# Layer 2 of a two-layer network: the loads of B and C become steps of the written plan, and one pair of states changes engine

## The chip, the core and the metric

The kernel runs on one core of one Trainium2 chip. The core has five engines that work side by side, each through its own queue of instructions in order: PE (TensorE, matrix products and transposes), DVE (VectorE), ACT (ScalarE), POOL (GpSimd) and SP (SyncE, which here only issues DMAs). The metric is the device time of one execution in microseconds (us); less is better.

## The reference

The input is an image batch of 4 x 192 x 128 x 128. Two layers follow one another, each with a residual sum over a group norm. Layer 1 is a convolution block in a fractional Fourier domain. It takes the first 1400 us or so, and the change doesn't touch it. Layer 2 is a selective state space model over the 16384 pixels of each image, with 384 channels and 16 states per channel:

```
xz = einsum(seq, in_proj_w);  xs, z = split(xz)
u = silu(causal_conv(xs, 4 taps))
dt, Bm, Cm = split(einsum(u, x_proj_w));  dt = softplus(dt_proj(dt))
for every token t:
    h = h * exp(dt_t * A) + (dt_t * u_t) * B_t        # 384 x 16 numbers
    y_t = sum over the 16 states of h * C_t
out = out_proj((y + u * Dp) * silu(z))
```

## The kernel before

Layer 2 cuts each image into 32 chunks of T = 512 tokens, 128 chunks in all. The 384 channels are three tiles of 128 partitions (j = 0, 1, 2), and the 16 states are eight pairs (sg = 0 to 7). One *group* is one j and one pair: 24 groups per chunk, k = 8 j + sg. The main loop runs over all groups of all chunks in order, `order` in the code, at position `pos`.

For one group the work is:

- the *decay* exp(dt A), one ACT activation per state (`decay`, L906)
- the *product* dt u B, made in one of three ways that the table `KINDS` names, a letter for each j and sg. V: DVE multiplies a copy of dt u in PSUM by B (`product`, L927). O: POOL multiplies both states at once (`inputs`, L938). P: dt u is transposed on PE (`turned`, L947), ACT scales the transposed blocks by B, which is a value per partition there (`scale`, L955, four activations per state), and PE transposes them back (`turned_back`, L970, four transposes per state)
- the *scan*, h = h x decay + product along the tokens, one DVE instruction per state (L984)
- the multiplication by C of both states at once on POOL (L997, hc)
- the sum over states on PE, by transposes that accumulate in PSUM (`sums`, L1010), three groups later (`LAG`)

After each group's scans SP issues a 1 KB DMA that keeps the last column of h for the next chunk (`carry`, L995).

The buffers matter. h has three (a scan of group k + 3 needs the buffer of group k: its hc and its carry DMA must be done). The PSUM ring `op` has three: each state uses one slot, for a V product, a turned-back P product, or the decay of an O state (`decay_there`, issued three states ahead). Decays of V and P states go to a ring of seven in SBUF (`early`). The scaled tiles dbT have four buffers, db two. For B and C there is one buffer per pair and kind, b0 to b6 and c0 to c7. Each holds two rows of 512 tokens spread to 128 partitions, 512 KB to move. B is not loaded for pairs that are P for all three j (sg 3 and 7).

All other work of a chunk, from the loads of x to the output projection, is written out by hand in `PLAN` (L560): a step is (position, phase, name, arguments). Positions count groups from the chunk's first scan. So the steps of the next chunk at -24 to -1 fall beside the scans of this one, at position + 24, and those from 24 on fall beside the scans of the next. The phases of one position are S, A, M, L: S first, then a turned-back product and the sums; A; then POOL's db product of two groups later; then the first scan, the next products, M, the second scan, and L. Within one engine the order of issue is the order of execution.

Steps named below: `evacuate` copies the sum of one j to SBUF (ACT), `turn` transposes it (PE), `gate` multiplies by silu(z) (DVE, L1042), `project_out` (PE) and `add_x` (DVE, L1056) finish the chunk. `to_tokens`, `moments`, `normed`, `to_channels`, `channels`, `conv`, `proj_z`, `silu_u`, `silu_z` and `proj_x` prepare a later one; `xd_out` and `dbc_out` store B and C to DRAM; `proj_dt`, `softplus` and `dt_u` (POOL, L853) make dt and dt u; `turn_b` and `b_out` make the transposed B.

The loads of B and C are the exception: they aren't in the plan. `load_bc` is called at the end of fixed positions, for pairs 0 to 4 in the last five groups of the chunk before and for pairs 5 to 7 in the first three groups:

```
if k >= NGR - BCL and n + 1 < total:
    load_bc(n + 1, k - (NGR - BCL))
if k < NG - BCL and n:
    load_bc(n, k + BCL)
```

Of the kernel before, what the change touches and what calls it, by code (L numbers as in the profile page):

```python
# [10 lines left out]
F32 = mybir.dt.float32  # L11
# [3 lines left out]
ALU = mybir.AluOpType  # L15
# [3 lines left out]
S = 128  # L19
# [4 lines left out]
L = S // 2 + 1  # L24
# [6 lines left out]
T = 512  # L31
# [90 lines left out]
def layer0(tc, x, xmid, st2, w):  # L122
# [432 lines left out]

BUFS = 7, 3

KINDS = ("VOPPVVOP", "VOVPVVPP", "VOVPVPOP")

PLAN = (  # L560
    (-35, "M", "load_x"), (-34, "L", "to_tokens", 0), (-33, "S", "to_tokens", 1),
    (-32, "S", "moments", 0), (-32, "L", "moments", 1), (-32, "L", "rstd"), (-30, "A", "shift"),
    (-30, "A", "normed", 0), (-30, "A", "normed", 1), (-30, "M", "to_channels", 1),
    (-28, "S", "to_channels", 0), (-28, "S", "channels", 0), (-27, "M", "conv", 0, 0),
    (-27, "L", "channels", 1), (-26, "A", "conv", 1, 0), (-25, "S", "conv", 1, 1),
    (-25, "A", "conv", 1, 2), (-21, "S", "conv", 0, 1), (-21, "L", "conv", 0, 2),
    (-20, "S", "silu_u", 0), (-20, "A", "silu_u", 1), (-19, "L", "conv", 2, 0),
    (-18, "S", "conv", 2, 1), (-18, "L", "conv", 2, 2), (-16, "L", "silu_u", 2),
    (-15, "A", "proj_z", 0), (-15, "M", "silu_z", 0), (-13, "M", "proj_x"), (-12, "S", "xd_out"),
    (-11, "M", "proj_dt"), (-10, "S", "dbc_out"), (-10, "A", "softplus", 0),  # L570
    (-10, "M", "softplus", 1), (-10, "M", "softplus", 2), (-10, "L", "turn_b"),
    (-10, "L", "b_out"), (-9, "L", "dt_u", 1), (-8, "L", "dt_u", 0), (-3, "L", "turned", 0),
    (-2, "M", "dtu_copy", 0), (-2, "L", "scale", 0, 6), (-1, "S", "scale", 0, 4),
    (0, "L", "scale", 0, 5), (1, "M", "scale", 0, 14), (2, "A", "scale", 0, 7),
    (3, "A", "scale", 0, 15), (4, "L", "turned", 1), (5, "M", "scale", 1, 6),
    (6, "S", "dtu_copy", 1), (7, "S", "scale", 1, 7), (7, "L", "dt_u", 2),
    (9, "M", "scale", 1, 14), (10, "M", "scale", 1, 13), (10, "L", "scale", 1, 15),
    (10, "L", "evacuate", 0), (10, "L", "proj_z", 1), (11, "M", "proj_z", 2),
    (11, "M", "silu_z", 1), (11, "M", "silu_z", 2), (11, "L", "scale", 1, 12),
    (11, "L", "turn", 0), (12, "L", "gate", 0), (13, "M", "dtu_copy", 2), (16, "M", "turned", 2),  # L580
    (17, "A", "scale", 2, 6), (17, "L", "scale", 2, 10), (18, "S", "scale", 2, 7),
    (18, "A", "evacuate", 1), (19, "S", "scale", 2, 14), (19, "A", "scale", 2, 11),
    (19, "L", "scale", 2, 15), (21, "A", "turn", 1), (21, "M", "gate", 1),
    (26, "M", "evacuate", 2), (28, "M", "load_xr"), (28, "L", "turn", 2), (30, "L", "gate", 2),
    (31, "S", "project_out", 0), (32, "L", "add_x", 0), (34, "S", "project_out", 1),
    (34, "L", "add_x", 1),
)


def layer1(tc, xmid, out, st2, w, n_tok=S * S):  # L590

    nc = tc.nc
    B = len(xmid)
    NCHUNK = n_tok // T
    G = 2
    LAG, BCL = 3, 5
    AHEAD, H = BUFS
    NBLK = T // 128

    with ExitStack() as ctx:  # L600
# [8 lines left out]
        bcp = pool("l1b", 1)  # L609
# [50 lines left out]
        for half in range(2):  # L660
            nc.sync.dma_start(
                out=wc[64 * half : 64 * (half + 1)], in_=w["taps"][half].partition_broadcast(64)
            )
        for part in range(2):
# [7 lines left out]
        xpT, dtT, dtb, cb, dp, woT, A = (  # L672
            const(k) for k in ("xpT", "dtT", "dtb", "cb", "dp", "woT", "A_log")
        )
# [8 lines left out]
        total = B * NCHUNK  # L683
        NG = NS // G
        NGR = NJ * NG
        got = [{} for _ in range(total)]
# [180 lines left out]
            )  # L867
            done(g, "bt")

        def load_bc(i, sg):  # L870

            g = got[i]
            if any(kinds[sg] != "P" for kinds in KINDS):
                t = g["b", sg] = bcp.tile([128, G, T], F32, name=f"b{sg}")
                nc.sync.dma_start(
                    out=t, in_=g["dbc"][0, sg * G : (sg + 1) * G, :].partition_broadcast(128)
                )
            t = g["c", "b", sg] = bcp.tile([128, G, T], F32, name=f"c{sg}")
            nc.sync.dma_start(
                out=t, in_=g["dbc"][1, sg * G : (sg + 1) * G, :].partition_broadcast(128)  # L880
            )

        def dtu_copy(n, j):

# [9 lines left out]
        def kind(k):  # L894
            return KINDS[k // NG][k % NG]

# [75 lines left out]
        def scans(pos, n, k, between):  # L972
            g = got[n]
            j, sg = divmod(k, NG)
            ch = n % NCHUNK
            if k == 0:
                g["carry"] = tp.tile([128, NJ, NS], F32, name="carry")
                g["before"], last["carry"] = last.get("carry"), g["carry"]
            db = g.pop(("db", k), None)
            h = scp.tile([128, G, T], F32, name="h", bufs=H)  # L980
            for q in range(G):
                st = sg * G + q
                s = G * pos + q
                nc.vector.tensor_tensor_scan(  # L984
                    h[:, q, :], das.pop(s), dbs.pop(s) if db is None else db[:, q, :],
                    0.0 if ch == 0 else g["before"][:, j, st : st + 1], ALU.mult, ALU.add,
                )
                product(s + 2)
                decay_there(s + 3)
                if q == 0:  # L990
                    turned_back(s + 3)
                    between()
                if s in turns:
                    early(turns[s] + AHEAD)
            nc.sync.dma_start(out=g["carry"][:, j, sg * G : (sg + 1) * G], in_=h[:, :, T - 1])  # L995
            hc = scp.tile([128, G, T], F32, name="hc", bufs=5)
            nc.gpsimd.tensor_tensor(hc, h, g["c", "b", sg], ALU.mult)  # L997
            g["hc", k] = hc

        def sums(n, k):  # L1000
# [53 lines left out]
        def add_x(n, t):  # L1054
# [6 lines left out]

        order = [(n, k) for n in range(total) for k in range(NGR)]
        does = dict(
            load_x=load_x, load_xr=load_xr, to_tokens=to_tokens, moments=moments, rstd=rstd, shift=shift,
            normed=normed, to_channels=to_channels, channels=channels, conv=conv, proj_z=proj_z,
            silu_u=silu_u, silu_z=silu_z, proj_x=proj_x, xd_out=xd_out, dbc_out=dbc_out, proj_dt=proj_dt, softplus=softplus, dt_u=dt_u,
            turn_b=turn_b, b_out=b_out, dtu_copy=dtu_copy, turned=turned, scale=scale,
            evacuate=evacuate, turn=turn, gate=gate, project_out=project_out, add_x=add_x,
# [14 lines left out]
        with tc.manual_schedule():  # L1083
            log_exp()
            for pos in range(first, 0):
                for phase in "SAML":
                    act(pos, phase)
                if pos == -8:
                    for sg in range(NG):
                        load_bc(0, sg)  # L1090
                if pos <= LAST:
                    yield pos == LAST
                if pos == LAST:
                    scp = pool("l1s", 4)
                    op = pool("l1o", 1)
                    ps2 = pool("l1q", 1, space=PSUM)
                    psa = pool("l1a", 3, space=PSUM)
                    banks.append(4)
                    group_norm(B - 1)
            inputs(*order[1])  # L1100
            for at in range(AHEAD):
                early(at)
            for s in range(2):
                product(s)
            decay_there(2)


            for pos, (n, k) in enumerate(order):
                j, sg = divmod(k, NG)
                act(pos, "S")  # L1110
                turned_back(G * (pos + 1))
                if pos >= LAG and sg != LAG:
                    sums(*order[pos - LAG])
                act(pos, "A")
                if pos + 2 < len(order):
                    inputs(*order[pos + 2])
                scans(pos, n, k, lambda: act(pos, "M"))
                act(pos, "L")
                if pos >= LAG and sg == LAG:
                    sums(*order[pos - LAG])  # L1120
                    add_skip(n, j)
                if k >= NGR - BCL and n + 1 < total:
                    load_bc(n + 1, k - (NGR - BCL))
                if k < NG - BCL and n:
                    load_bc(n, k + BCL)
            for pos in range(len(order), len(order) + end - NGR + 1):
                act(pos, "S")
                if pos < len(order) + LAG:
                    sums(*order[pos - LAG])
                for phase in "AML":  # L1130
                    act(pos, phase)
# [150 lines left out]
```

## Time and profile before

| | us |
|---|---|
| median of three runs | 11220.84 (11219.14 to 11226.6) |
| the profiled execution, its own time | 11219.08 |
| its span, first to last instruction | 11217.3 |
| granted TensorE clock, mean | 0.944 |
| hc on POOL (L997), one instruction | 2.367, 3072 times |
| scan on DVE (L984), one instruction | 1.267, 6144 times in four forms |
| V product on DVE (L927) | 0.675, 2560 times |
| carry DMA, issue to landing, median | 1.9 |
| loads of c and b, issue to landing, median | 6.0 and 5.0 |

In the rows of the profile, "L984 DVE" is the line of the code and the engine; the shapes are output <- input; "x" is a count; after the bar come the busy time in us and the mean length of one in ns; then the engine's idle time just before these instructions and what ended it. A wait list has one row for each engine, tile and releaser: the total in us, the number of times, and the longest. A timeline row begins with the start and the length in us, and ends in square brackets with the idle time ahead of it. A table of stretches has the stretch, its length, the busy time and the count of each engine, the granted clock, the mean busy share of the 16 DMA engines and the GB/s.

### The profile page before, as it was taken

The page shows a single profiled execution, that of the slowest core. Times are in us where ns is not written, and L with a number is a line of the kernel's source. Part 1 is how long each engine was busy: PE and PEld are TensorE (multiplying, and loading weights), DVE is VectorE, ACT ScalarE, POOL GpSimd, SP SyncE. Part 2 cuts the span into 40 slices and gives each one's busy share as a digit, 9 for nine tenths or more (in the row PEclk, how much of TensorE's full clock was granted, in tenths as well). Part 3 has the DMA queues.
Part 4 walks back from the last instruction along what each step waited for, and adds up shares of the span by engine and source line. Part 5 has one row for each costly group of instructions (what it writes and reads, how often), then busy time and mean ns, then how long its engine had stood idle before and what let it go on. Part 6 is the DMA issues. An engine that isn't in the chain of part 4 may idle for free. (4 is left out here: it accounts for less than half of the span.)

```text
span 11217.3 us, 171938 instructions
## 1 busy us (share of the span) xinstructions
PE 10022.3 (89%) x56050; PEld 7046.3 (63%) x56050; DVE 10265.6 (92%) x11587; ACT 9573.1 (85%) x20327; POOL 9223.7 (82%) x4214
## 2 busy tenths in 40 slices
PE   4777799999999999999999999999999999999998
PEld 2444366666666666666666666666666666666666
DVE  5667599999999999999999999999999999999999
ACT  2333299999999999999999999999999999999998
POOL 0000199999999999999999999999999999999998
PEclk8888799999999999999999999999999999999999
DMA  8886734334334334334344334344344344344343
GB/s 233 191 226 180 225 96 123 112 111 123 113 110 123 109 114 123 107 117 123 105 119 123 105 118 123 102 121 123 100 121 124 99 123 123 99 124 121 101 123 96
DMA packets 1357326, 1416.85 MB, mean 126 GB/s; under 512 B 920729, under 2 KB 972174, under 8 KB 1355790
## 3 DMA queue, kind: packets, MB, share of 16 engines
q1 hardware_dynamic: 1335950, 1342.94, 41.5%
q0 software_dynamic: 13312, 50.34, 1.4%
q10 hardware_dynamic: 7168, 12.59, 0.3%
q8 instruction: 446, 7.31, 0.3%
q14 instruction: 450, 3.69, 0.1%
HBM read 1230.12 MB, written 155.33 MB: 124 GB/s over the span
## 5 line engine op out<-in xcount | busy, mean ns | idle before, releaser
L997 POOL TENSOR_TENSOR hc<-h,c 128x1024 f32<-128x1024 f32 x3072 | 7218.1, 2367 | 691.6 <-DVE h L984 572.5
L984 DVE TENSOR_TENSOR_SCAN h<-da,carry,op 128x512 f32<-128x512 f32 x4712 | 5846.4, 1267 | 157.3 <-PE op L970 78.9
L906 ACT ACTIVATE da<-dt,c_A_log 128x512 f32<-128x512 f32 x4864 | 3394.9, 737 | 75.4 <-DVE h L984 68.0
L1010 PE MATMUL ps<-ident,hc 128*128 128x128 f32 x24576 | 3270.7, 281 | 5.7 <-POOL hc L997 4.8
L1010 PEld LDWEIGHTS ps<-ident,hc 128*128 128x128 f32 x24576 | 2919.1, 146 | 279.4 <-issue 257.4
L955 ACT ACTIVATE dbT<-ps,bT 128x128 f32<-128x128 f32 x9216 | 2547.7, 389 | 2.7 <-PE ps L947 2.7
L795 PE MATMUL ps<-s,wc 128*128 128x512 f32 x4608 | 2141.1, 596 | 57.1 <-ACT s L780 57.1
L970 PE MATMUL op<-ident,dbT 128*128 128x128 f32 x9216 | 1500.7, 288 | 612.3 <-DVE h L984 588.2
L970 PEld LDWEIGHTS op<-ident,dbT 128*128 128x128 f32 x9216 | 1137.6, 148 | 1004.8 <-ACT dbT L955 556.0
L927 DVE TENSOR_TENSOR op<-ps,b 128x512 f32<-128x512 f32 x2560 | 1727.2, 675 | 6.4 <-ACT ps L887 1.0
L984 DVE TENSOR_TENSOR_SCAN h<-op,carry,db 128x512 f32<-128x512 f32 x1240 | 1542.3, 1269 | 109.1 <-DMA carry<-h 51.3
L938 POOL TENSOR_TENSOR db<-dtu,b 128x1024 f32<-128x1024 f32 x640 | 1515.0, 2367 | 6.1 <-DVE nmr L638 6.1
L795 PEld LDWEIGHTS ps<-s,wc 128*128 128x128 f32 x4608 | 806.6, 191 | 761.2 <-issue 684.8
L906 ACT ACTIVATE op<-dt,c_A_log 128x512 f32<-128x512 f32 x1280 | 906.7, 708 | 219.8 <-DVE h L984 219.3
L1049 PE MATMUL ps<-yg,c_woT 128*96 128x512 f32 x1536 | 710.8, 599 | 2.1 <-ACT u L807 0.9
L692 ACT ACT_TABLE_LOAD x511 | 655.6, 1283 | 10.0 <-PEq L1272 0.7
L514 POOL DMA_DIRECT2D xmid<-xt x64 | 42.1, 658 | 585.6 <-DVE xt L510 557.1
L1049 PEld LDWEIGHTS ps<-yg,c_woT 128*96 128x96 f32 x1536 | 241.3, 163 | 429.7 <-issue 312.5
L853 POOL TENSOR_TENSOR dtu<-dt,u 128x512 f32<-128x512 f32 x384 | 489.9, 1276 | 0.0
L1019 ACT COPY yt<-ps 128x512 f32<-128x512 f32 x384 | 226.4, 590 | 283.0 <-PE ps L1010 282.2
L1025 PE MATMUL ps<-ddp,u 128*128 128x128 f32 x3072 | 446.1, 293 | 0.0
L205 DVE BATCH_NORM_STATS2 st<-xt 96x6 f32<-96x512 f32 x512 | 322.5, 677 | 104.5 <-DMA xt<-in_x 103.4
(173 smaller groups left out, 9609.5 us busy)
## 6 DMA issues: line engine op xcount, KB each, us to landing
c<-dbc SPq DMA_DIRECT2D x1024, 512.0 KB, 6.0
b<-dbc SPq DMA_DIRECT2D x768, 512.0 KB, 5.0
xt<-in_x SPq DMA_DIRECT2D x176, 768.0 KB, 8.4
xmid<-xt POOLq DMA_DIRECT2D x64, 768.0 KB, 6.1
xm<-xmid SPq DMA_DIRECT2D x128, 384.0 KB, 3.7
carry<-h SPq DMA_DIRECT2D x3072, 1.0 KB, 1.9
xr<-xmid SPq DMA_DIRECT2D x128, 384.0 KB, 4.9
out<-xr SPq DMA_DIRECT2D x128, 384.0 KB, 3.3
```

The source lines that it names most:

```text
L692: nc.scalar.preload_act_table_set("natural_log_exp_and_others")
L795: nc.tensor.matmul(g["c", j][0], wc[:, j, k, :], rhs, start=k == 0, stop=k == 5)
L853: nc.gpsimd.tensor_tensor(g["dtu", j], g["dt", j], g["u", j], ALU.mult)
L906: nc.scalar.activation(da, got[n]["dt", j], AF.Exp, scale=A[:, j, st : st + 1])
L927: nc.vector.tensor_tensor(dbs[s], g["dp", j][0], g["b", k % NG][:, q, :], ALU.mult)
L938: nc.gpsimd.tensor_tensor(db, _bc(g["dtu", j], 1, G), g["b", sg], ALU.mult)
L955: nc.scalar.activation(t[:, blk, :], g["tu", j][0][:, at], AF.Identity, scale=g["bT"][:, blk, st : st + 1],)
L970: nc.tensor.transpose(db[:, blk * 128 : (blk + 1) * 128], t[:, blk, :], ident)
L984: nc.vector.tensor_tensor_scan(h[:, q, :], das.pop(s), dbs.pop(s) if db is None else db[:, q, :], 0.0 if ch == 0 else g["before"][:, j, st ...
L997: nc.gpsimd.tensor_tensor(hc, h, g["c", "b", sg], ALU.mult)
L1010: nc.tensor.matmul(py[:, blk, :], hc[:, q, blk * 128 : (blk + 1) * 128], ident, start=first, stop=sg == NG - 1 and q == G - 1 and blk == N ...
L1049: nc.tensor.matmul(g["po", t][0][0:CH], woT[:, j, t * CH : (t + 1) * CH], g["yg", j], start=j == 0, stop=j == NJ - 1,)
```

## The change

Three things are edited together. `load_bc` is split into `load_b` and `load_c`, and each call becomes a step of the plan. In the plan before the loads ran at groups 19 to 23 and 0 to 2 (end of the position). In the new one, in positions from the chunk's first scan: b0 at -7; b2, b1, c0 at -6; c1, b4, c2, c3 at -4; b5 at -1; c4, c6 at 0; b6 at 1; c5 at 2; c7 at 5 (steps for b3 and b7 load nothing). One letter of `KINDS` goes from P to O: j = 1, sg = 6. So a chunk has six O, ten V and eight P pairs instead of five, ten and nine. And the order of nearly all other steps in the plan is new.

```diff
-KINDS = ("VOPPVVOP", "VOVPVVPP", "VOVPVPOP")
+KINDS = ("VOPPVVOP", "VOVPVVOP", "VOVPVPOP")
```

```diff
 PLAN = (
...
-    (-30, "A", "normed", 0), (-30, "A", "normed", 1), (-30, "M", "to_channels", 1),
-    (-28, "S", "to_channels", 0), (-28, "S", "channels", 0), (-27, "M", "conv", 0, 0),
...
-    (-18, "S", "conv", 2, 1), (-18, "L", "conv", 2, 2), (-16, "L", "silu_u", 2),
...
-    (-11, "M", "proj_dt"), (-10, "S", "dbc_out"), (-10, "A", "softplus", 0),
-    (-10, "M", "softplus", 1), (-10, "M", "softplus", 2), (-10, "L", "turn_b"),
-    (-10, "L", "b_out"), (-9, "L", "dt_u", 1), (-8, "L", "dt_u", 0), (-3, "L", "turned", 0),
-    (-2, "M", "dtu_copy", 0), (-2, "L", "scale", 0, 6), (-1, "S", "scale", 0, 4),
-    (0, "L", "scale", 0, 5), (1, "M", "scale", 0, 14), (2, "A", "scale", 0, 7),
...
-    (18, "A", "evacuate", 1), (19, "S", "scale", 2, 14), (19, "A", "scale", 2, 11),
-    (19, "L", "scale", 2, 15), (21, "A", "turn", 1), (21, "M", "gate", 1),
...
-    (31, "S", "project_out", 0), (32, "L", "add_x", 0), (34, "S", "project_out", 1),
-    (34, "L", "add_x", 1),
+    (-30, "M", "normed", 0), (-29, "S", "normed", 1), (-29, "M", "to_channels", 0),
+    (-29, "M", "channels", 0), (-26, "S", "conv", 1, 0), (-26, "S", "to_channels", 1),
...
+    (-17, "L", "conv", 2, 1), (-15, "A", "conv", 2, 2), (-15, "L", "proj_z", 0),
+    (-15, "L", "silu_z", 0), (-14, "M", "silu_u", 2), (-13, "M", "proj_x"), (-11, "S", "xd_out"),
+    (-10, "A", "dbc_out"), (-10, "A", "proj_dt"), (-10, "A", "softplus", 0),
+    (-10, "L", "softplus", 1), (-9, "S", "softplus", 2), (-9, "S", "turn_b"), (-9, "M", "b_out"),
+    (-9, "L", "dt_u", 0), (-7, "A", "load_b", 0), (-7, "L", "dt_u", 1), (-6, "S", "load_b", 2),
+    (-6, "S", "load_b", 1), (-6, "A", "load_c", 0), (-5, "M", "turned", 0),
+    (-4, "S", "load_c", 1), (-4, "S", "load_b", 4), (-4, "L", "load_c", 2),
+    (-4, "L", "load_c", 3), (-3, "S", "load_b", 3), (-2, "A", "scale", 0, 7),
+    (-2, "M", "dtu_copy", 0), (-2, "M", "scale", 0, 15), (-1, "S", "load_b", 5),
+    (-1, "M", "scale", 0, 6), (-1, "M", "scale", 0, 4), (0, "M", "load_c", 4),
+    (0, "L", "load_c", 6), (1, "S", "scale", 0, 5), (1, "M", "load_b", 6), (2, "A", "load_b", 7),
+    (2, "L", "load_c", 5), (3, "S", "scale", 0, 14), (5, "A", "turned", 1), (5, "A", "load_c", 7),
...
+    (18, "S", "scale", 2, 10), (18, "S", "scale", 2, 6), (18, "L", "evacuate", 1),
...
+    (21, "M", "turn", 1), (21, "M", "gate", 1), (25, "S", "load_xr"), (27, "A", "evacuate", 2),
+    (28, "L", "turn", 2), (31, "A", "gate", 2), (32, "M", "project_out", 0),
+    (33, "A", "add_x", 0), (34, "S", "project_out", 1), (35, "S", "add_x", 1),
 )
```

```diff
-        def load_bc(i, sg):
-            g = got[i]
+        def rows_of(i, name, sg):
+            t = got[i][name, sg] = bcp.tile([128, G, T], F32, name=f"{name}{sg}")
+            a = "bc".index(name)
+            nc.sync.dma_start(
+                out=t, in_=got[i]["dbc"][a, sg * G : (sg + 1) * G, :].partition_broadcast(128)
+            )
+
+        def load_b(i, sg):
             if any(kinds[sg] != "P" for kinds in KINDS):
...
+                rows_of(i, "b", sg)
+
+        def load_c(i, sg):
+            rows_of(i, "c", sg)
...
-                if pos == -8:
-                    for sg in range(NG):
-                        load_bc(0, sg)
...
-                if k >= NGR - BCL and n + 1 < total:
-                    load_bc(n + 1, k - (NGR - BCL))
-                if k < NG - BCL and n:
-                    load_bc(n, k + BCL)
```

## The prediction

> **What bounds the kernel now.** I read the page first, for the busy shares and the costliest groups; then the busy time over a steady stretch of layer 2; then the DVE's waits in that stretch; then the POOL's timeline over part of one chunk, to see where it is free.
>
> ```profile
> PE 10022.3 (89%) x56050; PEld 7046.3 (63%) x56050; DVE 10265.6 (92%) x11587; ACT 9573.1 (85%) x20327; POOL 9223.7 (82%) x4214
> ...
> L955 ACT ACTIVATE dbT<-ps,bT 128x128 f32<-128x128 f32 x9216 | 2547.7, 389 | 2.7 <-PE ps L947 2.7
> ...
> L970 PE MATMUL op<-ident,dbT 128*128 128x128 f32 x9216 | 1500.7, 288 | 612.3 <-DVE h L984 588.2
> ...
> L938 POOL TENSOR_TENSOR db<-dtu,b 128x1024 f32<-128x1024 f32 x640 | 1515.0, 2367 | 6.1 <-DVE nmr L638 6.1
> ```
>
> Shares over the whole span mix the two layers; layer 2 starts near 1400 us. Its steady stretch (busy us and counts of PE, PEld, DVE, ACT, POOL, then clock, DMA share, GB/s) and three pieces of one chunk:
>
> ```profile
> 2000.00:11000.00 9000.00, 8339.51 (x48363) 6001.20 (x48362) 8629.94 (x9622) 8448.74 (x18194) 8369.99 (x3760) 0.96 0.39 115
> 5063.00:5089.00 26.00, 25.64 (x151) 19.28 (x150) 21.26 (x21) 22.77 (x58) 23.02 (x10) 0.95 0.82 269
> 5089.00:5124.00 35.00, 33.42 (x176) 21.36 (x174) 34.96 (x38) 33.10 (x62) 31.16 (x14) 1.00 0.22 50
> 5124.00:5142.00 18.00, 13.80 (x93) 12.08 (x91) 17.53 (x27) 16.63 (x38) 17.34 (x10) 0.78 0.06 4
> ```
>
> The store of dbc is issued once per chunk, first at 1339.2 and last at 11097.6 us: 9758.4 / 127 = 76.84 us per chunk, so 9000 us are 117.1 chunks. Per chunk DVE is busy 8629.94 / 117.1 = 73.7 us, ACT 72.1, POOL 71.5 and PE 71.2. DVE, with 3.16 us idle, is the bound, and everything else is within 4% of it: only DVE's idle time can be won. What its idle time waited for, 2000 to 11000 us:
>
> ```profile
> DVE yg L1042 <- PE ps L1035: 105.1, 116, 1.3
> DVE h L984 <- PE op L970: 75.7, 188, 0.5
> DVE h L984 <- DMA carry<-h: 68.0, 89, 2.4
> DVE h L984 <- issue: 45.7, 52, 1.5
> DVE h L984 <- ACT dbT L955: 31.4, 24, 1.7
> DVE h L984 <- ACT da L906: 14.0, 26, 0.9
> DVE h L984 <- POOL hc L997: 10.4, 11, 2.1
> ```
>
> Divided by 117.1: the gate for PE 0.90 us per chunk, scans for a turned-back P product 0.65, for a carry DMA (which holds one of three h buffers) 0.58, unnamed 0.39, scaled tiles 0.27, decays 0.12, POOL 0.09; together 3.0. So nine tenths are waits for PE, ACT and DMA, not for POOL. Where POOL is free, groups 10 to 15 of one chunk:
>
> ```profile
> 5031.90 2.37 POOL L997 TENSOR_TENSOR hc<-h,c 128x1024 f32<-128x1024 f32 x1 [0.54 <-DVE h L984]
> 5035.51 2.35 POOL L997 TENSOR_TENSOR hc<-h,c 128x1024 f32<-128x1024 f32 x1 [1.24 <-DVE h L984]
> 5039.07 2.37 POOL L997 TENSOR_TENSOR hc<-h,c 128x1024 f32<-128x1024 f32 x1 [1.21 <-DVE h L984]
> 5043.14 2.36 POOL L997 TENSOR_TENSOR hc<-h,c 128x1024 f32<-128x1024 f32 x1 [1.69 <-DVE h L984]
> 5045.80 2.37 POOL L997 TENSOR_TENSOR hc<-h,c 128x1024 f32<-128x1024 f32 x1 [0.30 <-DVE h L984]
> ```
>
> These gaps add up to 4.98 us (3.42 in the next chunk), waiting for scans.
>
> **What the Trainium skill says.** "DMA: Bandwidth & Descriptors", Queues, rings and completion order: SP owns one ring on each DMA engine, and an engine takes descriptors in ring order. So a 1 KB carry issued behind 512 KB loads starts after them; the trace agrees, carries land after 1.9 us in the median and 7.6 at most. "GPSIMD Engine Reference", 3.1 Elementwise: about 2.6 cycles per element for a two-input operation at 1.2 GHz, an estimate of 2.2 us for 1024 elements; the trace has 2.37. "ScalarE: Activation LUTs", What ACT_TABLE_LOAD costs: 1283 ns a load and another 1380 of draining. The trace has the 1283, but the activation after the load of 5013.02 starts at 5014.32, so no draining shows; 1.28 us is the price.
>
> **The pair that changes kind (j=1, sg=6, from P to O).** Removed per chunk: two scales of four activations, 8 x 2547.7/9216 = 2.2 us of ACT, and eight transposes, 8 x 1500.7/9216 = 1.3 us of PE. ACT falls to 69.9 us, PE to 69.9. Added: one db product. Back to back they start 2.33 us apart in the timeline: POOL rises to 73.8. DVE runs the same 48 scans (1269 against 1267 ns by the form of their inputs) and 20 products: nothing changes there. The two decays move from the SBUF ring filled seven states ahead to the PSUM ring of three, issued three states ahead; ACT then waits for a scan as the other O decays do (196.7 us over 10 such decays per chunk, about 0.17 each). That is 0.3 us of ACT, inside the 2.2 it saves. The new db is queued on POOL ahead of group 12's hc, in the hole shown above (3.4 to 5.0 us against 2.33), so no h buffer comes free late there. And groups 14 and 15, today both P, make the recurring 0.47 us wait of group 15's first scan (as at 5046.12 and 5124.88); with 14 an O this goes. Nearly hidden on POOL, worth about 0.4 us per chunk on DVE.
>
> **The loads.** Fourteen loads of 512 KB per chunk, unchanged in number. Today they leave from group 19 to group 2 of the next chunk, two at a time: DMA is at 0.82 there against 0.06 just before. The carry waits lie in and just behind that stretch (5086.40: 1.89 us). After: one at group 17, three at 18, four at 20, one at 23, two at 0, one each at 1, 2 and 5. 7.3 MB over some 40 us would be 183 GB/s, an estimate, against the 269 measured in the 26 us shown above. Each load's buffer was last read two or more groups earlier, so SP shouldn't block, and carries behind it on SP aren't held. The tightest is c5, issued at the end of group 2 and used at group 5, near 7 us later against a landing of 6. Bunches are at most two loads ahead of one carry, about 4 us, and an h buffer is wanted two groups (4.7 us or more) after its carry is issued. I take 0.58 to 0.1 us; bounds 0 and 0.6.
>
> **The order.** The yg wait is at group 21: before it PE was held at to_channels by ACT, which waited for evacuate(1) at group 18 (ACT waited 249.9 us for sums, 2.1 per chunk). Now evacuate(1) is the last step of group 18, behind normed(0), and the to_channels come at 19 and 22. But turn(1) and gate(1) now are neighbours in the same phase of group 21, and PE still has a turned-back product and the sums ahead of turn(1). I take the gate from 0.90 to 0.5 and the unnamed wait before it from 0.39 to 0.25. Scans behind P products: 0.65 to 0.3, by the removed 0.47 and with something given back at group 11: there PE gets conv(2,1) at 7 and conv(2,2) at 9 between two P pairs, one convolution step of four matmul records (1.72 us) more than now, in a stretch where PE already is busy for 11.88 of 11.90 us (5098.40 to 5110.30), and add_x(1) now comes before group 11's scans and waits for the same PE. Two more waits are new: scale(0,5) at group 1 finds four dbT tiles alive and must wait for the first of them to be turned back; behind it ACT's decays queue, which are seven states ahead. And proj_dt moves from 13 to 14, the three softplus share one table load across 14 and 15 (no SBUF decay is issued in group 14 any more), and b_out and the decays of group 17 queue behind them. Loads of tables stay at eight a chunk. For ACT's waits on DVE I take 0.39 to 0.3; bounds of the whole reorder minus 1.2 and plus 1.5 us.
>
> **Sum.** POOL now has 73.8 us of its own against DVE's 73.7: two nearly full engines coupled by three h buffers; I allow 0.4 us for DVE waiting on hc. Gate 0.5, P products 0.3, carry 0.1, unnamed 0.25, dbT and decays 0.3, POOL 0.4: 1.85 us against 3.02, 1.17 less. The period is 75.7 us. Over 127 chunks that is 149 us; layer 1, the start and the tail I cost at nothing, since fill and drain follow the same path. From the profiled execution's own 11219 us (span 11217.3 and 2 around it; the median is 11220.8, 2 more): 11070.
>
> **Rivals.**
> A. The waits all but go. Nothing is left but the POOL chain: 73.8 us and 0.5 of coupling, 74.3, times 127: minus 323, 10896. For it: the work removed from PE and ACT exceeds every wait on them. Against: four engines over 94%.
> B. The wait moves to PE between groups 6 and 11: there 1.0 us of the extra 1.72 shows, most of the gain: minus 0.2 us per chunk, 11194, from 11150 to 11260. For it: PE 25.6 of 26 and 33.4 of 35 us busy there. Against: it starts that stretch with less behind it.
> C. Slower: POOL becomes the bound. It has 73.8 us of work and 5.38 idle today, 4.4 of it waits for scans (519.9/117.1). If these keep 4.0 because hc must follow its own scan and db products and dt_u collect before hc at groups 15 to 20, the period is 77.8: plus 122, 11341. It decides from 3.05 us of POOL idle per chunk on. For it: H stays 3, and a new db lengthens POOL's chain. Against: the hole at 10 to 15 is right there, and DVE waited only 0.09 us for POOL.
>
> **Numbers.** Forecast 0.52 (own range 10990 to 11140), A 0.15, B 0.14, C 0.19. 0.2% is 22 us, about what a measurement can tell. B gives 0.05 faster, 0.05 same, 0.04 slower; C 0.02 same, 0.17 slower. Faster 0.72, same 0.07, slower 0.21. The range takes in A and the lower side of B and C: 10890 to 11250.
>
> **What would show it.** Right: POOL 128 instructions more, ACT and PE 1024 fewer; carry waits under 25 us over the steady stretch; DMA share flat where it was 0.82; no 0.47 at group 15; DVE at 97.5% or more. Wrong: POOL idle above 3 us per chunk with DVE waiting on hc (C); L970 or add_x waits at group 11 above 0.7 us per chunk (B); ACT waits at groups 1 or 17 that end scans late.

## The result and the profile after

The new kernel takes 11137.58 us in the median of four runs (11122.07 to 11148.63), against 11219.99: a ratio of 0.9926, with a 95% interval from 0.9909 to 0.9943. That is 82 us less, where 149 were forecast. The profiled execution took 11134.09 us, 85 less than the one before.

The first view is the page's busy times and two rows of its DMA part, of the new kernel. POOL has 128 instructions more, PE and ACT have 1024 fewer, as the change of one pair asks, and both loads now land after 4.7 us (6.0 and 5.0 before).

```profile
PE 9935.4 (89%) x55026; PEld 6973.1 (63%) x55026; DVE 10209.6 (92%) x11587; ACT 9346.5 (84%) x19303; POOL 9523.9 (86%) x4342
...
c<-dbc SPq DMA_DIRECT2D x1024, 512.0 KB, 4.7
b<-dbc SPq DMA_DIRECT2D x768, 512.0 KB, 4.7
```

The second is the steady stretch, in the columns used for the kernel before.

```profile
2000.00:11000.00 9000.00, 8324.54 (x47750) 5974.81 (x47748) 8640.18 (x9695) 8300.23 (x17377) 8706.37 (x3905) 0.96 0.41 116
```

DVE has 82 instructions per chunk, so 9000 us hold 9695 / 82 = 118.2 chunks, where they held 9622 / 82 = 117.3. But DVE's busy time has risen by 10 us only: per chunk it is still idle for 3.04 us (3.15 before). What it waited for, in the same stretch:

```profile
DVE h L988 <- DMA carry<-h: 131.4, 128, 2.7
DVE st L731 <- PE ps L716: 116.5, 118, 2.3
DVE yg L1046 <- PE ps L1039: 103.7, 114, 1.3
DVE xr L1060 <- PE ps L1053: 3.3, 7, 0.9
DVE h L988 <- PE op L974: 1.7, 5, 0.6
```

Per chunk that is 1.11 us for carries (0.58 before), 0.99 for the group-norm statistics, a wait that wasn't there, 0.88 for the gate (0.90), and almost nothing for P products (0.65) and for POOL. The list of reasons changed and the total did not.

To see where in a chunk this lies I took the starts of all 6144 scans and the idle time ahead of each DVE instruction from the trace, and averaged over chunks 10 to 123 by group. This table is worked out so; it is no view of the profile.

| per chunk, us | before | after |
|---|---|---|
| period, scan to scan | 76.65 | 76.12 |
| idle ahead of group 1 / 3 / 4 | 0.84 / 0.19 / 0 | 0 / 0 / 1.07 |
| idle at 15 | 0.47 | 0 |
| idle at 16, ahead of the statistics | 0 | 0.97 |
| idle at 21, gate and the scan before it | 1.24 | 0.95 |
| idle at 23 | 0.23 | 0 |
| all idle time of DVE | 3.13 | 3.05 |
| instructions' own lengths, summed | 79.85 | 79.54 |

Idle time and lengths make up 0.39 of the 0.53 us that a chunk is shorter by. The remaining 0.14 is overlap: a DVE instruction that waited for nothing starts about 0.085 us before the end of the one ahead of it, and there are 3.3 interruptions of more than 0.05 us per chunk instead of 5.7. So the idle time itself fell by 0.08 us only. For the shorter lengths I have no cause. In the runs below the sum lies between 79.5 and 79.9 without any order.

The third view is the timeline of the new kernel at the three places that hold the waits: group 1 with its transfers and group 4's first scan; group 16; group 21.

```profile
5041.64 0.56 SPq L876 DMA_DIRECT2D c<-dbc  x1
5042.25 0.42 SPq L707 DMA_DIRECT2D xr<-xmid  x1
5042.73 0.45 SPq L876 DMA_DIRECT2D b<-dbc  x1
...
5043.30 2.94 SPq L999 DMA_DIRECT2D carry<-h  x2
...
5050.55 1.28 DVE L988 TENSOR_TENSOR_SCAN h<-da,carry,op 128x512 f32<-128x512 f32 x1 [1.40 <-DMA carry<-h]
...
5010.41 1.85 ACT L849 ACTIVATE dt<-ps,c_dtb 128x512 f32<-128x512 f32 x3
...
5011.15 0.66 PE L951 MATMUL ps<-ident,dtu 128*128 128x128 f32 x4 [0.97 <-ACT dt L849]
...
5013.10 1.03 PE L716 MATMUL ps<-gd,xm 97*128 97x96 f32 x8
...
5014.17 0.63 DVE L731 BATCH_NORM_STATS2 st<-ps 128x6 f32<-128x192 f32 x2 [0.62 <-PE ps L716]
...
5030.18 0.60 PE L1039 MATMUL ps<-ident,yt 128*128 128x128 f32 x4
...
5030.82 0.69 DVE L1046 TENSOR_TENSOR yg<-ps,zs 128x512 f32<-128x512 f32 x1 [0.86 <-PE ps L1039]
```

At group 1 three transfers go out within 1.1 us, c6, xr and b6, and the carry behind them. It lands 6.8 us after its issue on average (5.0 before), and group 4's scan needs its buffer. At group 16 the transposes of `turned` wait on PE for a PSUM bank that a softplus holds, `turn_b`, sums and `to_tokens` are queued behind, and the statistics wait for the last. At group 21 `turn` ends at 5030.78, and the gate starts 0.04 us later.

One more thing stands ahead of group 21, in both kernels: the granted TensorE clock. In most chunks it falls to half in groups 17 to 20, for 3.4 us or two or three times that; on average for 5.7 us per chunk before and 4.9 after. In the kernel before, PE waits for 3.96 us ahead of one such stretch, and the four transposes that follow take 1.08 us, where the same four took 0.60 ten microseconds earlier:

```profile
5125.39 0.60 PE L970 MATMUL op<-ident,dbT 128*128 128x128 f32 x4
...
5135.48 1.08 PE L970 MATMUL op<-ident,dbT 128*128 128x128 f32 x4 [3.96 <-DVE h L984]
```

DVE's idle time in groups 21 to 23 goes with it. These are chunks 10 to 123, sorted by their time at half clock in groups 17 to 20 (worked out from the traces; the last column is a kernel of the next section):

| at half clock, us | before: chunks, idle us | after | both parts, old order |
|---|---|---|---|
| 0 | 4, 0.20 | none | 34, 0.34 |
| 3.4 | 61, 1.09 | 65, 0.82 | 53, 0.95 |
| 6.8 | 17, 1.38 | 49, 1.12 | 18, 1.50 |
| 10.2 | 32, 2.50 | none | 9, 2.61 |

So a good part of what is named for PE at groups 21 to 23, the gate above all, goes with the clock and not with the order of the steps alone. That is an association: no run set the clock. What precedes such a stretch is an idle PE. In the last column's kernel PE and its weight loads are busy for 19% of the 3.4 us ahead of it, on average of 80 such stretches, where the median of all pieces of that length is 100%.

### The profile page after: what moved, and what is told of

Its sections match the earlier page's. It is cut to its first block, busy times and chain, and to the rows that moved or that the text cites. A ratio compares the mean times of both kernels' runs of the same rounds, so it can differ in the third digit from the quotient of the medians.

```text
span 11132.3 us, 168105 instructions
## 1 busy us (share of the span) xinstructions
PE 9935.4 (89%) x55026; PEld 6973.1 (63%) x55026; DVE 10209.6 (92%) x11587; ACT 9346.5 (84%) x19303; POOL 9523.9 (86%) x4342
## 4 chain that ended last, share of the span: by engine, by line
PE 46%; ACT 23%; DVE 15%; issue 5%; DMA 2%; POOL 0%; SPq 0%; DVEq 0%; POOLq 0%; ACTq 0%
PE ps L1014 12%; PE ps L798 12%; DVE h L988 10%; ACT da L910 8%; PE op L974 7%; PE ps L1053 6%; ACT L695 4%; DVE op L931 3%; ACT op L910 3%; ACT dbT L959 2%; PE ps L951 1%; ACT L810 1%; ACT u L810 1%; PE ps L767 1%; DMA carry<-h 1%
## 5 line engine op out<-in xcount | busy, mean ns | idle before, releaser
L988 DVE TENSOR_TENSOR_SCAN h<-da,carry,op 128x512 f32<-128x512 f32 x4464 | 5526.6, 1262 | 137.9 <-DMA carry<-h 134.5
L910 ACT ACTIVATE da<-dt,c_A_log 128x512 f32<-128x512 f32 x4608 | 3251.1, 737 | 239.6 <-DVE h L988 221.4
L1014 PE MATMUL ps<-ident,hc 128*128 128x128 f32 x24576 | 3315.0, 281 | 4.5 <-POOL hc L1001 4.5
L959 ACT ACTIVATE dbT<-ps,bT 128x128 f32<-128x128 f32 x8192 | 2274.6, 397 | 0.0
L974 PE MATMUL op<-ident,dbT 128*128 128x128 f32 x8192 | 1456.4, 300 | 628.8 <-ACT dbT L959 478.1
L988 DVE TENSOR_TENSOR_SCAN h<-op,carry,db 128x512 f32<-128x512 f32 x1488 | 1837.6, 1262 | 2.0 <-ACT da L910 1.1
L942 POOL TENSOR_TENSOR db<-dtu,b 128x1024 f32<-128x1024 f32 x768 | 1820.8, 2371 | 6.1 <-DVE nmr L641 6.1
L974 PEld LDWEIGHTS op<-ident,dbT 128*128 128x128 f32 x8192 | 1037.7, 149 | 1144.8 <-ACT dbT L959 534.8
L910 ACT ACTIVATE op<-dt,c_A_log 128x512 f32<-128x512 f32 x1536 | 1084.2, 706 | 167.4 <-DVE h L988 166.5
L817 ACT ACTIVATE zs<-ps 128x512 f32<-128x512 f32 x384 | 229.4, 597 | 304.6 <-PE ps L805 304.6
```

The lines of the kernel that those rows point to most:

```text
L910: nc.scalar.activation(da, got[n]["dt", j], AF.Exp, scale=A[:, j, st : st + 1])
L942: nc.gpsimd.tensor_tensor(db, _bc(g["dtu", j], 1, G), g["b", sg], ALU.mult)
L959: nc.scalar.activation(t[:, blk, :], g["tu", j][0][:, at], AF.Identity, scale=g["bT"][:, blk, st : st + 1],)
L974: nc.tensor.transpose(db[:, blk * 128 : (blk + 1) * 128], t[:, blk, :], ident)
L988: nc.vector.tensor_tensor_scan(h[:, q, :], das.pop(s), dbs.pop(s) if db is None else db[:, q, :], 0.0 if ch == 0 else g["before"][:, j, st ...
L1014: nc.tensor.matmul(py[:, blk, :], hc[:, q, blk * 128 : (blk + 1) * 128], ident, start=first, stop=sg == NG - 1 and q == G - 1 and blk == N ...
```

## The experiments

Ratios are to the kernel before as it was measured again beside each run, with 95% intervals. Its medians lie between 11220 and 11227 us, so a difference between two rows can be off by some 7 us.

| kernel | median us | ratio | period us |
|---|---|---|---|
| old order, pair changed (pair_alone) | 11083.97 | 0.9872 [0.9858, 0.9885] | 75.64 |
| old order, loads moved (loads_alone) | 11011.91 | 0.9805 [0.9791, 0.9818] | 75.09 |
| old order, both (pair_and_loads) | 10881.84 | 0.9690 [0.9677, 0.9703] | 74.11 |
| new order, pair changed, old loads (old_loads) | 11239.58 | 1.0011 [1.0002, 1.0019] | 76.87 |
| new order, loads moved, old pair (old_kinds) | 12307.56 | 1.0959 [1.0944, 1.0974] | 85.27 |
| the same, scales and softplus rearranged (old_kinds_2) | 11332.39 | 1.0092 [1.0078, 1.0105] | 77.65 |
| new kernel, load_xr later (xr_later) | 11008.89 | 0.9803 [0.9789, 0.9816] | 75.08 |
| that, with statistics and gate later (all_three) | 11011.51 | 0.9802 [0.9789, 0.9815] | 75.09 |
| xr_later, turned(2) later (turned_later) | 10954.80 | 0.9762 [0.9748, 0.9775] | 74.79 |
| xr_later, two conv steps earlier (conv_earlier) | 10964.08 | 0.9767 [0.9754, 0.9781] | 74.81 |
| pair_and_loads, load_xr at group 1 (pl_xr) | 11043.19 | 0.9843 [0.9829, 0.9856] | 75.37 |
| pair_and_loads, gate later (pl_gate) | 10861.05 | 0.9680 [0.9667, 0.9693] | 73.95 |

**The two parts in the old order.** The pair alone:

```diff
-KINDS = ("VOPPVVOP", "VOVPVVPP", "VOVPVPOP")
+KINDS = ("VOPPVVOP", "VOVPVVOP", "VOVPVPOP")
-    (9, "M", "scale", 1, 14), (10, "M", "scale", 1, 13), (10, "L", "scale", 1, 15),
+    (9, "M", "scale", 1, 14), (10, "L", "scale", 1, 15),
-    ... (11, "L", "scale", 1, 12),
```

> The kernel before with one letter changed: j=1, sg=6 from P to O, its two scales gone, everything else in the old order with the old loads. My theory (the parts each take waits away, the new order puts others in their place): the 0.47 us wait of group 15's first scan goes, the waits at groups 1, 3 and 21 stay; POOL's new product hides in its hole at groups 10 to 15. About 0.5 us per chunk, 63 us less: 11155 (ratio 0.9945). Rival (POOL is the floor, a new product lengthens its chain): no gain, 11220 or more, with DVE waiting on hc. Rival (the pair carries the whole gain): 11138.

142 us less, more than twice what was expected. The 0.47 us at group 15 went, as did the slack around it: the stretch from group 13 to 15 takes 8.99 us instead of 9.80, and groups 20 and 21 together take 0.2 us less. Whether PE's or ACT's relief did it isn't separated. The gain is larger than that of the whole change, so both the theory's number and the rivals fell.

The loads alone, at the new kernel's positions, with the rest of the plan as before:

```diff
+    (-7, "A", "load_b", 0), (-6, "S", "load_b", 2), (-6, "S", "load_b", 1), (-6, "A", "load_c", 0),
+    (-4, "S", "load_c", 1), (-4, "S", "load_b", 4), (-4, "L", "load_c", 2), (-4, "L", "load_c", 3),
+    (-1, "S", "load_b", 5), (0, "M", "load_c", 4), (0, "L", "load_c", 6), (1, "M", "load_b", 6),
+    (2, "L", "load_c", 5), (5, "A", "load_c", 7),
```

> The kernel before with the fourteen loads at the new kernel's positions; kinds and all other steps as before, so load_xr stays at 28 (group 4). My theory: the carry waits at groups 1 and 3 (0.84 and 0.19 us per chunk) go, nothing else: some 0.7 us per chunk, 90 us less: 11130 (0.992). Rival (loads are hidden anyway, the order did it): 11215 to 11225. Rival (the bunches of the new positions themselves make carries late): a carry wait of about 1 us at group 4 here too, and 11200 or more.

214 us less. The wait list of this kernel, 2000 to 11000 us, has carries at 9.5 us where the kernel before had 68.0 and the new one 131.4:

```profile
DVE yg L1047 <- PE ps L1040: 105.9, 91, 5.8
DVE h L989 <- PE op L975: 88.2, 222, 1.5
DVE h L989 <- DMA carry<-h: 9.5, 18, 0.8
```

Groups 0 and 2 took 3.27 and 2.57 us and take 2.36 and 2.34. That is 1.14 of the 1.56 us per chunk, twice what the rows named carry had shown: waits at group 1 that had other names, or none, were those of late carries too. In the trace of the kernel before, 50 waits of more than 0.15 us ahead of the first scans of groups 1 and 3 have the landing of the carry three groups back on record. Each ends 0.12 us after that landing, whether the row names the carry, a decay, a scaled tile or POOL, and the hc of that group had ended 1.9 us before or more.

Both together:

> The kernel before with both the changed pair and the moved loads, but with its own order. My theory (the two gains sit at different groups, 1 and 3 against 15, and add; the new order loses): the periods add, 76.65 - 1.01 - 1.56 = 74.1 us per chunk, 325 us less than before: 10895 (0.971), and DVE's waits are those at 16, 21 and 23 alone. Rival (POOL with 73.6 us is a floor with coupling): no better than the loads alone, 11000. Rival (the order is needed for the two to go together): 11100 or more.

Exactly the sum: the period is 74.11 where 74.1 was expected. This kernel ends at 10884 us, so its steady stretch is taken from 2000 to 10800. The stretch and DVE's waits in it:

```profile
2000.00:10800.00 8800.00, 8201.22 (x47941) 5871.48 (x47940) 8674.01 (x9733) 8322.85 (x17449) 8725.62 (x3924) 0.98 0.41 119
```

```profile
DVE yg L1047 <- PE ps L1040: 62.8, 77, 1.3
DVE h L989 <- PE op L975: 36.6, 105, 1.8
DVE h L989 <- DMA carry<-h: 13.0, 26, 1.4
...
DVE h L989 <- POOL db L943: 1.6, 2, 0.9
...
DVE h L989 <- POOL hc L1002: 0.6, 2, 0.3
```

POOL is busy for 8725.62 of 8800 us, 99.2%, and DVE waits for it for 2.2 us in all. So POOL doesn't hold this period up, but it is now the busiest engine, and only 0.6 us per chunk are left above its own work. With both parts the new order costs 0.9926 / 0.9690 = 1.024: 256 us.

**The new order without one of the parts.** The loads back at the ends of groups 19 to 23 and 0 to 2, everything else as in the new kernel:

```diff
+                if k >= NGR - BCL and n + 1 < total:
+                    load_bc(n + 1, k - (NGR - BCL))
+                if k < NG - BCL and n:
+                    load_bc(n, k + BCL)
```

> The new kernel (new order, changed pair) with the loads where they were: two at a time at the ends of groups 19 to 23 and 0 to 2. My theory (load position and order are separate losses): carries are late again around groups 0 to 3, now with load_xr at group 1 in the middle of them, while 16 and 21 keep their waits: 50 to 150 us more than the new kernel, 11190 to 11290. Rival (the new order was right and only the loads' new places hurt it): below 11060.

As expected. Group 4's wait is 1.19 us here, and carries of groups 1 and 2 land after 7.1 and 7.3 us, with load_xr among the old loads. No run has the old loads in the new order and load_xr at 28, so its share here isn't separated. The loads' new places are worth 0.9% in the new order, against 1.9% in the old one.

The pair back at P in the new order:

```diff
-KINDS = ("VOPPVVOP", "VOVPVVOP", "VOVPVPOP")
+KINDS = ("VOPPVVOP", "VOVPVVPP", "VOVPVPOP")
-    (7, "M", "scale", 1, 14), (9, "M", "scale", 1, 15), (10, "L", "proj_z", 1),
+    (7, "M", "scale", 1, 14), (9, "M", "scale", 1, 15), (10, "M", "scale", 1, 13), (11, "L", "scale", 1, 12), (10, "L", "proj_z", 1),
```

> The new kernel with j=1, sg=6 back at P, and its two scales at 10 and 11. My theory: the 0.4 to 0.5 us wait at groups 14 and 15 comes back, POOL falls to 71.5 us per chunk, the waits at 4, 16 and 21 stay: 55 us more than the new kernel, 11190 (0.9975). Rival (POOL is the floor): faster than the new kernel, below 11130. Rival (PE is late in 6 to 15): clearly more than before, over 11230.

A miss by 1100 us, and no clean test of the pair. With group 14 a P pair its decays are issued between the softplus steps again, so that the softplus need two table loads a chunk instead of one, each followed by a load for the decays. ACT's loads in one such place (start, length):

```profile
5013.27 1.28 ACT L849 ACT_TABLE_LOAD   x1
5015.57 1.28 ACT L695 ACT_TABLE_LOAD   x1
5018.21 1.28 ACT L849 ACT_TABLE_LOAD   x1
5021.63 1.28 ACT L695 ACT_TABLE_LOAD   x1
```

The bank that softplus holds comes free late, and the first statistics wait for 6.1 us per chunk; the scale at 11 is late too and costs 2.8 us at group 14. So the number asked for by the last rival came out, by way of the tables and not of PE. The softplus steps of the new plan stand on the changed pair. With them in one phase, and the scales earlier:

```diff
-    (7, "M", "scale", 1, 14), (9, "M", "scale", 1, 15), (10, "L", "proj_z", 1),
+    (7, "M", "scale", 1, 12), (9, "M", "scale", 1, 13), (11, "S", "scale", 1, 14),
+    (12, "S", "scale", 1, 15), (10, "L", "proj_z", 1),
-    (-10, "L", "softplus", 1), (-9, "S", "softplus", 2),
+    (-10, "M", "softplus", 1), (-10, "M", "softplus", 2),
```

> The new kernel with the pair back at P once more, now with its scales issued at 7 and 9, those of the next pair at 11 and 12, and the three softplus in one phase of group 14, so that they share one table load (at 12307 us the run before had three loads there and scales that came late). My theory: the P pair costs the new order about what it costs the old one, 1.0 us per chunk: 11260, with a wait at groups 14 or 15. Rival (the new order can't hold nine P pairs: PE late from group 11 on): over 11400.

Between the two, 1.7% above the new kernel, and softplus and scales moved with it. DVE waits for 0.74 us at group 14, as expected, and also for 0.62 at add_x(1) and 0.55 at group 19. The expectation's "three loads" were two. With the softplus together the wait at 16 is nearly gone (0.05 us for the first statistics); but DVE comes there later, after the waits at add_x and group 14.

**The three places of the new order.** load_xr first:

```diff
-    (25, "S", "load_xr"),
+    (28, "M", "load_xr"),
```

> The new kernel with load_xr back at 28 (group 4, phase M) from 25 (group 1, phase S), where it goes out between c6 and b6 ahead of group 1's carry. My theory: carry(1), which lands 6.8 us after its issue, lands in 4 to 5, and group 4's wait of 1.07 us per chunk falls to 0.2 or less: 0.9 us per chunk, 110 us less than the new kernel, 11030 (0.983). Rival (POOL's 73.6 us and its coupling hold the period, the wait moves to hc): at most 30 us less, 11110. Rival (b6 and c6 alone make carry(1) late): the wait at 4 stays above 0.7, 11120.

129 us less than the new kernel. Carry(1) lands after 4.7 us instead of 6.8, and DVE's waits for carries are 4.2 us in the steady stretch. The counterpart, the same step moved the other way in the old order with both parts:

```diff
-    (26, "M", "evacuate", 2), (28, "M", "load_xr"), (28, "L", "turn", 2),
+    (26, "M", "evacuate", 2), (25, "S", "load_xr"), (28, "L", "turn", 2),
```

> The old order with changed pair and moved loads (10882 us), and of the new order one step alone: load_xr at 25 (group 1, phase S) instead of 28. My theory (384 KB between c6 and b6, ahead of carry(1), cost the new kernel its wait at group 4): the wait of about 1 us at group 4 appears and 0.9 to 1.1 us per chunk are lost: 11010 (0.981). Rival (that wait needs the rest of the new order): below 10910.

It costs 161 us, and group 4's wait is back at 0.96 us, 122 us over 127 chunks; carry(1) lands after 6.7. The rest goes with longer waits at group 21, 0.99 us per chunk against 0.74. One load of 384 KB at the wrong place is settled as the cause of that wait, in either order.

Next the statistics and the gate, each one phase later, with load_xr at 28:

```diff
-    (-32, "M", "moments", 0),
+    (-32, "L", "moments", 0),
-    (21, "M", "gate", 1),
+    (21, "L", "gate", 1),
```

> The new kernel with three steps moved: load_xr at 28 again, moments(0) from phase M to L of group 16, gate(1) from phase M to L of group 21. My theory (the new order loses by three places alone): the waits of 1.25 us at 16 and 0.76 us at 21 fall below 0.2 each, so the period goes from 75.1 (load_xr alone) to 73.5 to 74.1: 10830 to 10900, as good as the old order with both parts. Rival (POOL floor): the waits move to hc or POOL's idle stays, 10990. Rival (what the gate and the statistics waited for is late for something else): one of them shows up at the next group, 10950 or more.

No gain over load_xr alone. The gate's wait went, and 0.59 us appeared at group 23, where a V product waits for the copy of dt u to PSUM (68.1 us in the steady stretch, on ACT). The statistics' wait was split and stayed in sum, 1.27 us: 0.52 for the first step, and 0.75 for the second, which stands behind to_tokens(1). So covering the consumer moved both waits on; what they wait for is late.

What is late? PE's wait for a bank, ahead of to_tokens:

```diff
-    (15, "S", "turned", 2),
+    (16, "M", "turned", 2),
```

> The new kernel with load_xr at 28 (11009 us), and turned(2) back at 16, phase M, from 15, phase S. At 15 it takes a PSUM bank that a softplus still holds, and to_tokens(0), which group 16's statistics wait for, is queued behind it on PE. My theory: the wait of 1.25 us at 16 falls below 0.4, the gate's stays: 10900 to 10930. Rival (to_tokens is late because PE as a whole is late, softplus and turn_b before it): the wait stays over 0.9, 10980 or more.

Between the two: 0.75 us stay on average. But the chunks are of two kinds. In 64 of 114 the granted clock stays full from group 14 to the statistics, and the wait is 0.05 us; in 50 a stretch at half clock begins there, and the wait is 1.65. Two neighbouring chunks of this kernel, the 3.4 us up to the statistics (the clock is the third number from the end) and the statistics themselves:

```profile
5535.20:5538.60 3.40, 2.44 (x23) 2.42 (x23) 3.38 (x4) 3.37 (x6) 3.40 (x2) 1.00 0.14 18
5610.90:5614.30 3.40, 3.40 (x20) 3.40 (x18) 1.88 (x3) 3.37 (x6) 3.40 (x2) 0.52 0.04 0
...
5538.62 0.63 DVE L731 BATCH_NORM_STATS2 st<-ps 128x6 f32<-128x192 f32 x2
...
5614.31 0.63 DVE L731 BATCH_NORM_STATS2 st<-ps 128x6 f32<-128x192 f32 x2 [1.53 <-PE ps L716]
```

The same split in xr_later gives 69 chunks with 0.63 us and 45 with 2.18, and in the new kernel 89 with 0.63 and 25 with 2.20. So at full clock the theory holds: with turned(2) behind it to_tokens starts 0.55 us earlier, and the wait goes. The rest goes with the clock, which neither the theory nor the rival named.

PE's wait of 0.97 us for the bank, 113.0 us from 2000 to 10800 us in xr_later, is 113.9 us here, now ahead of turn_b: the softplus give it back late in both. ACT, which runs them, waits for 2.3 us per chunk at silu_z (270.8 us in that stretch of xr_later), for PE's proj_z. So, to make the softplus earlier, the two convolution steps went back to where the old order had them:

```diff
-    (-17, "L", "conv", 2, 1), (-15, "A", "conv", 2, 2), (-15, "L", "proj_z", 0),
+    (-18, "S", "conv", 2, 1), (-18, "L", "conv", 2, 2), (-15, "L", "proj_z", 0),
```

> The new kernel with load_xr at 28 (11009 us), and conv(2,1) and conv(2,2) back at group 6, phases S and L, from 7 and 9. Moving turned(2) left the 0.97 us wait for a bank on PE, which only went over to turn_b, so the softplus themselves are late. My theory: PE is late from group 6 to 11 by the convolution steps, so ACT waits 2.3 us per chunk at silu_z, its softplus come late, free their banks late, and to_tokens(0) and the statistics of group 16 with them. With the steps earlier the silu_z wait falls below 1.2 us and group 16's from 1.25 to under 0.5: 10890 to 10940. Rival (proj_dt at 14 and the softplus spread over 14 and 15 are late by their own places): group 16's wait stays over 0.9, 10980 or more.

Two of DVE's waits of this kernel, 2000 to 10800 us:

```profile
DVE xr L1060 <- PE ps L1053: 111.1, 118, 1.5
...
DVE st L731 <- PE ps L716: 4.1, 5, 2.1
```

The statistics' wait is gone, 145.5 us in xr_later and 4.1 here. But it didn't go by the chain that the expectation names. ACT's wait at silu_z fell to 204.8 us, 1.7 per chunk, where less than 1.2 was expected, and the softplus begin 46.5 us after the chunk's first scan, 46.4 in xr_later. What changed is DVE: it stops for 0.95 us at add_x(0), whose project_out stands behind the steps that were moved, so it comes to group 16 1.0 us later. And in 113 of 114 chunks the clock stays full up to the statistics, where it did in 69. Three quarters of the gain went back, and the total fell short of what was expected. That PE has too much to do in groups 6 to 11 isn't shown by this.

A plainer rival has no run. The old order has to_tokens(0) at the end of group 14 and the first statistics at the start of group 16; the new one has both in group 16, two phases apart.

**A better version.** The old order with both parts, and one more step:

```diff
-    (21, "A", "turn", 1), (21, "M", "gate", 1),
+    (21, "A", "turn", 1), (21, "L", "gate", 1),
```

> The old order with changed pair and moved loads (10882 us), and gate(1) at phase L of group 21 instead of M, behind the second scan. My theory: its 0.53 us and the 0.21 before it go, unless the bank that the gate frees is then missed by the copy of dt u for group 23, as it was with the new order: 10800 to 10830. Rival (the wait moves to group 23): 10870 to 10890.

The gate's wait went from 0.53 us to nothing, but groups 22 and 23 now wait for P products for 0.63 us instead of 0.18: 21 us less where 50 to 80 were expected, with intervals that overlap. So the rival's mechanism is what the trace shows, and the gain isn't clear of the noise. At 10861 us this has the lowest median of the kernels, 3.2% below the one before. Of its 0.92 us of idle DVE per chunk 0.86 lie in groups 21 to 23; in the 38 chunks without half clock in groups 17 to 20 only 0.23 do. POOL is busy for 8734.33 of 8800 us, so about 0.55 us per chunk can still be won before POOL's own work is the limit.

## Why the prediction came out as it did

The total lay inside the range and on the right side, but its sum was made of wrong terms. That it fell into the range is luck: the two parts gave more than was forecast, and the new order, forecast as a gain, took most of it back. Forecast and measured, us of DVE's waits per chunk: gate 0.50 and 0.88, P products 0.30 and 0.01, carries 0.10 and 1.11, unnamed 0.25 and 0, scaled tiles and decays 0.30 and 0.02, POOL 0.40 and 0, statistics 0 and 0.99.

- **The pair.** Counts, the hole on POOL and the end of group 15's wait were right. "Worth about 0.4 us per chunk on DVE" was mis-sized: alone in the old order it is worth 1.0.
- **The loads.** "I take 0.58 to 0.1 us" was right in mechanism and too small: moving the loads alone takes 1.56 us, since half of what late carries cost stood under other names.
- **The step that failed first:** "Bunches are at most two loads ahead of one carry". By the prediction's own list of positions three stand ahead of the carry of group 18; that one lands after 5.2 us, and DVE doesn't wait for it. What did harm is that I counted c and b only and didn't look at what else the new order sends through SP. load_xr moved from 28 to 25, into group 1. It is 384 KB between c6 and b6, costs 1.07 us of DVE's idle time and 129 us in all.
- **The order.** Forecast as a gain, it loses 2.4%, half of it by load_xr. The waits for P products and the unnamed ones fell further than forecast. The gate came out at 0.88, not 0.5: turn and gate as neighbours leave it no cover, and the half clock ahead of group 21, visible as 0.78 in the stretch from 5124 to 5142 us that the prediction shows, was in no term. Neither was the wait of the statistics: 0.63 us of it come from turned(2) ahead of to_tokens, the rest goes with the clock. Rival B had PE late in groups 6 to 11 by the convolution steps and looked for a wait at group 11; none came, and the run that moved these steps doesn't show that they made the wait at 16.
- **POOL.** The 0.4 us allowed for hc was not needed: 0.00 us in the new kernel, 0.01 in the best ones, with POOL busy for 96.7% in the new kernel and 99.2% in the best. Rival C fell with it.
- **ACT.** The two waits named there, scale(0,5) for a dbT buffer and the late proj_dt, hardly show as DVE waiting for ACT: rows with ACT as releaser are 1.8 us in the steady stretch. Whether the second acted by way of the bank is open; no run moved proj_dt alone.
- **A reading.** "Nine tenths are waits for PE, ACT and DMA" counts the unnamed 0.39 us with them: the named ones are 2.52 of 3.0 us. Of the signs of being right, the counts and group 15 came true; carries under 25 us (131.4) and DVE at 97.5% (96.0) did not.

The forecast was 1.17 us of shorter waits, and so of a shorter period. The period is 0.53 shorter, DVE's idle time only 0.08: the two parts gave 2.54 in the old order, and the new order took 2.0 of them back.

## What to carry to other kernels

When several steps of a hand-written order move at once, put the old order under each part first: here both parts were worth 3.1% together, and the reordering that came with them hid three quarters of it. For each queue, list all transfers between two that matter, not only those that the change names. A wait that moves to the next step when it is covered has its cause upstream: follow what the late producer itself waited for before moving the consumer. And where a wait comes and goes from chunk to chunk, sort the chunks before averaging: here one mean of 0.75 us was 0.05 at full clock and 1.65 at half.

## What the hardware showed

- A 1 KB DMA lands after 1.9 us in the median. Behind two loads of 512 KB the carry of group 1 took 4.6 to 5.0 us (4.7 in xr_later), and one 384 KB load more made it 6.7 to 6.8 (pl_xr, the new kernel): about 2 us for 0.39 MB. Behind three loads the carry of group 18 took 4.9 to 5.3.
- Interrupting DVE costs more than the idle time. In the kernel before, scans that follow without a wait start 0.086 us before the end of the one ahead and last 1.264 us; after a wait of more than 0.15 us there is no overlap and they last 1.279. That is about 0.1 us for each interruption, before a wait's own length.
- POOL ran its multiplications for 99.2% of the time without making DVE wait for more than 2.2 us in 8800 (pair_and_loads), with three h buffers between them.
- The granted TensorE clock went to half for 3.4 us or a multiple of it after PE had been mostly idle (19% busy in the 3.4 us ahead, 80 stretches of pair_and_loads), and four transposes then took 1.08 us instead of 0.60 (the kernel before).
